# A norm moved ahead of a product, and a feed-forward piece moved to the end of a slot, in a two-layer Perceiver kernel

## The chip, the cores and the metric

The kernel runs on one core of a Trainium2 chip. The metric is the device time of one execution in microseconds (us). The core has a matrix engine (TensorE, PE in the profile, with its weight loads as PEld), VectorE (DVE), ScalarE (ACT), GpSimd (POOL) and SyncE (SP), which issues most DMA transfers. Each engine has its own queue of instructions; semaphores order them between engines.

## The reference

Sixteen sequences of 64 tokens of width 256 (1024 tokens) go through two layers, all in float32. Each layer has a cross-attention over a context of 1601 rows of width 192, a self-attention or a stand-in for it, and a feed-forward part. Each step adds to the residual stream, and each takes a layer norm of it:

```
x = x + L0_xattn(layernorm(x), ctx)     # 16 heads of 16
x = x + L0_attn(layernorm(x))           # causal self-attention, see below
x = x + L0_ffn(layernorm(x))            # gelu, 256 -> 1024 -> 256
x = x + L1_xattn(layernorm(x), ctx)     # 8 heads of 64
x = x + L1_attn(layernorm(x))           # a scan of gradient steps over sequences
x = x + L1_ffn(layernorm(x))            # mixture of experts, top 2 of 8, and a shared one
```

The self-attention is the one of the first edit:

```
q, k, v from rmsnorm(x); 16 query heads, 8 key/value heads of 64
q, k = each head's row divided by its norm, times a scale     # "heads' norms"
sim = tanh(q k / 50) * 50 / 8, causal; attn = softmax(sim)
out = sum of the two query heads of a group (attn v), then @ Wout
```

## The kernel before

The 1024 tokens lie as eight tiles `x[t]` of 128 tokens (two sequences each) by 256. The program is written as one order of pieces; each piece emits instructions on several engines, and each engine runs its own in the order in which they were written. Blocks under `manual_schedule` are not reordered. Four stages follow each other: `cross0` (0 to about 820 us), `middle` (self-attention and the first feed-forward, 820 to 1019 us), `cross1` (the second cross-attention with the scan, the router and the last feed-forward tile between its matmuls), and `experts`.

**`middle`** loops over the eight tiles. One turn of the loop is a list of pieces that belong to three tiles at once: tile t's attention, tile t-1's feed-forward (`before`), and tile t+1's projections (`after`). What matters here:

- `project(after, n)`: the products for queries (n = 0, 1), keys (n = 2) and values (n = 3), line L137 (the helper that accumulates). For n < 3 ScalarE squares the result (L1820) and VectorE sums it (L1829).
- `inverse_norms(after)`: a root on ScalarE (L1833) and a reciprocal on VectorE, 24 heads at once.
- `over_norm(after, n)`: one product on VectorE (L1838, 128 x 512), in the order n = 2, 0, 1. The three results are read by `turn_keys` (L697), `turn_queries(t, 0)` and `turn_queries(t, 1)` (L711) at the start of the next turn of the loop.
- `attention_out(t)`: a product on TensorE and the addition to `x[t]` on VectorE (L795).
- `feed.norm2(t)`: the layer norm ahead of the feed-forward: statistics on VectorE (L1435, L1437, L627), a root on ScalarE (L109), a reciprocal (L110), the scaled tile `xs` (L1444), then a bias row that GpSimd adds to `x[t]` (L132). `feed.norm3` and `make.norm1` are the same for the next layer's norm and the next tile's first norm.
- `feed.turn2(before)` transposes norm2's `xs` on TensorE (L634) and copies it on ScalarE (L637, `xt`). It stands between the two `turn_queries`. `feed.hidden` reads `xt` (L137, 32 matmul records `h`) and ends in GELUs on ScalarE (L1875); `feed.out` is L1886 and its addition L1894; `turn1(after)` transposes the next tile's first norm (L634 again).

Tile 7's `norm2` and tile 6's `norm3` are not made in `middle`; they come at the start of `cross1`.

**`cross1`** goes through 64 units v (a sequence and a pair of heads each), one slot per unit. A slot holds, in this order on TensorE: two groups of transposes of the weights of unit v-1 (L991), the main part of the scores of v (L947), the other transposes, the rest of the scores (L959), whose maxima (L971, L972, L974) and exponentials (L977 to L979) `weights` emits on VectorE and ScalarE, and the weighted sum of v-1 (L1007). Three times in a slot other work is let in:

```
place_in(v, 3.9)                 # behind the main scores
place_in(v, 1.6, long=True)      # behind weights
place_in(v, 1.6)                 # behind the weighted sum
```

Outside the last nine slots `place_in` calls `place`, which takes the next piece of `feed` (a generator) as long as it has one, and after that a piece of the scan or the router. `feed` is `FeedForward.rest()`: norm2 of tile 7 and norm3 of tile 6 (emitted ahead of the first slot), then `turn3` + `turn2`, `hidden(0)`, `hidden(1)`, `out` with norm3 of tile 7, and `turn3`. So the first slot's three places hold `turn3` + `turn2`, `hidden(0)` and `hidden(1)`; there is no v-1 in this slot, so nothing else of it lies behind `weights`.

Of the kernel before, what the change touches and what calls it, by code (L numbers as in the profile page):

```python
# [76 lines left out]
class Perceiver:  # L77
# [561 lines left out]
    def middle(self, make):  # L639
# [6 lines left out]
        with ExitStack() as ctx:  # L646
# [35 lines left out]
            def projected(name):  # L682
                return ps_q.tile([P, 512], F32, tag="q", name=name)

            feed = FeedForward(
                self, sb, psum, lambda: ps_y.tile([P, D], F32, tag="y", name="y")
            )
# [127 lines left out]
            def each(*pieces):  # L815

                for f, t, *more in pieces:
                    if 0 <= t < NT and (f, t) not in ((feed.norm2, last), (feed.norm3, last - 1)):
                        f(t, *more)

            with tc.manual_schedule():
                for t in range(NT):
                    before, after = t - 1, t + 1
                    first = last if t == 0 else NT

                    end, soon, later = (t, before, NT) if t == last else (NT, NT, before)
                    each(
                        (turn_keys, t),
                        (turn_queries, t, 0),
                        (last_of_cross0, first, 0),  # L830
                        (feed.turn2, before),
                        (turn_queries, t, 1),
                        (last_of_cross0, first, 1),
                        (feed.norm3, before - 1),
                        (make.norm1, after if t else NT),
                        (feed.hidden, before, 0),
                        (feed.hidden, before, 1),
                        (turn1, after),
                        (scores, t),
                        (feed.turn3, before - 1),  # L840
                        (feed.out, before, 0),
                        (project, after, 2),
                        (next_queries, end, -1, 0),
                        (attend, t),
                        (project, after, 0),
                        (feed.out, soon, 1),
                        (join, t),
                        (project, after, 1),
                        (next_queries, end, 0, 3),
                        (make.inverse_norms, after),  # L850
                        (make.over_norm, after, 2),
                        (make.over_norm, after, 0),
                        (attention_out, t),
                        (next_queries, end, 3, 6),
                        (make.over_norm, after, 1),
                        (feed.norm2, t),
                        (project, after, 3),
                        (feed.out, later, 1),
                        (next_queries, end, 6, 8),
                    )  # L860
                    if t == 2:
                        self.load_context(0)
# [48 lines left out]
    def cross1(self, ps_m, scan, shared, one, early):  # L911
# [7 lines left out]
        with ExitStack() as ctx:  # L919
# [7 lines left out]
            def turned(name):  # L927
# [3 lines left out]
            feed = FeedForward(  # L931
                self,
                sb,
                turned,
                lambda: ps_m.tile([P, D], F32, tag="tr", name="y"),
                ("at", "at", "pt", "p"),
            ).rest()
# [45 lines left out]
            def transposed(v, n):  # L983

                if n == 0:
                    pts[v] = sb.tile([P, NCH, P], F32, tag="pt", name="pt")
                ks = range(4 * n, min(4 * n + 4, NCH))
                w = chunk_rows(ks[0])
                t = ps_w.tile([P, 4, P], F32, tag="w", name="w")
                for k in ks:  # L990
                    nc.tensor.transpose(  # L991
                        t[:w, k - ks[0], :], ps[v][:, k * P : k * P + w], self.ident
                    )
                copy = nc.scalar.copy if n % 2 else nc.vector.tensor_copy
                copy(pts[v][:w, ks[0] : ks[-1] + 1, :], t[:w, : len(ks), :])  # L995
# [18 lines left out]
            def over_weights(v):  # L1014
                den = self.small.tile([P, 1], F32, tag="den1", name="den1")
                nc.vector.reciprocal(den, us[v][:, DC:])
                nc.vector.tensor_scalar(us[v][:, :DC], us[v][:, :DC], den, None, ALU.mult)

            def sums_by_width(v):
                b, j = divmod(v, 4)  # L1020
                if v % 8 == 0:
                    uts[b // 2] = self.early.tile([DH, 2, 8, 2, N], F32, tag="ut", name="ut")
                m = ps_m.tile([DH, 2, P], F32, tag="tr", name="m")
                for i in range(2):
                    nc.tensor.transpose(m[:, i, :], us[v][:, i * DH : (i + 1) * DH], self.ident)
                for i in range(2):
                    self.evacuate(
                        uts[b // 2][:, i, 2 * j : 2 * j + 2, b % 2, :],
                        m[:, i, :].rearrange("p (e q) -> p e q", e=2),
                    )  # L1030
# [23 lines left out]
            def place(long=False):  # L1054

                if next(feed, False) is False:
                    scan.go_on(long=long)

            def last_slots(v):
                return v >= units - 9  # L1060

            def place_in(v, us, long=False):

                if last_slots(v):
                    scan.timed(us)
                else:
                    place(long)
# [11 lines left out]
            def first_half():  # L1079
                next(first, None)  # L1080

            def table():
                nonlocal made
                if made is None:
                    made = self.table(one, *TABLES[0], self.counts[NT - 2], True)
                self.first_table = next(made)
# [5 lines left out]
            for v in range(units + 2):  # L1092
                if 0 <= v - 1 < units:
                    transposed(v - 1, 0)
                if 0 <= v - 2 < units:
                    over_weights(v - 2)
                if 0 <= v - 1 < units:
                    transposed(v - 1, 1)
                if v >= units:
                    first_half()  # L1100
                    sums_by_width(v - 2)
                if v > units:

                    table()
                    first_half()
                    values(NT - 1)
                    table()
                    first_half()
                    first_half()
                    output(NT - 1)  # L1110
                    scan.timed(3.0)
                    table()
                    for _ in range(3):
                        first_half()
                        scan.timed(0.9)
                    break
                if v < units:
                    scores_main(v)
                    if 0 <= v - 2:
                        sums_by_width(v - 2)  # L1120
                place_in(v, 3.9)
                if 0 <= v - 1 < units:
                    transposed(v - 1, 2)
                    transposed(v - 1, 3)
                if last_slots(v):
                    scan.timed(0.7)
                if v >= units:
                    first_half()
                t, m = divmod(v + 6, 8)
                if t < NT and m == 0:  # L1130
                    self.queries(t, turned)
                if t < NT and 1 <= m < 5:
                    self.queries_by_width(t, 2 * (m - 1), turned)
                if v < units:
                    scores_rest(v)
                    weights(v)
                if t < NT and 1 <= m < 5:
                    self.queries_by_width(t, 2 * (m - 1) + 1, turned)
                t, m = divmod(v - 9, 8)
                if 0 <= t < NT - 1 and m == 0:  # L1140
                    values(t)
                if 0 <= t < NT - 1 and m == 1:
                    output(t)
                place_in(v, 1.6, long=True)
                if 0 <= v - 1 < units:
                    weigh(v - 1)
                place_in(v, 1.6)
                if v == units:
                    table()
                if v % 4 == 1 and 0 < v < units - 4:  # L1150
                    self.load_context((v + 3) // 4)
                if v == 1:
                    early()

# [979 lines left out]
```

## Time and profile before

| what | value |
|---|---|
| median of three runs | 2147.42 us (2143.57, 2147.42, 2154.95) |
| profiled execution | 2142.42 us |
| its span, first to last instruction | 2140.8 us |
| mean granted TensorE clock | 0.992 |
| PE busy | 2074.3 us, 97% of the span |
| DVE busy | 1114.3 us, 52% |
| ACT busy | 682.4 us, 32% |
| POOL busy | 152.4 us, 7% |
| one tile of `middle` (from one turn_keys to the next) | 25.98 us |

The profile's line numbers are those of the kernel. `L634 MATMUL t<-ident,xs` is an instruction of line 634 that writes the tile t and reads ident and xs. In rows in order of time the first number is the start in us from the span's start, the second the length, and a bracket at the end gives the idle time of the engine just before and what ended it. A helper's line (L137, L634, L637, L1444) stands for all its callers, so position and tile names tell which one it is. A clock of 1.00 is full speed.

### The profile page before, as it was taken

The numbers are of one execution on the slowest core, as the hardware profiler recorded it, in microseconds if no ns is written. First come the engines' busy times: TensorE is split into PE (matmuls) and PEld (weight loads), VectorE is DVE, ScalarE is ACT, GpSimd is POOL, SyncE is SP. The second block draws the span as 40 slices with busy tenths as digits, with TensorE's granted clock in tenths as the row PEclk, the third lists the DMA queues.
The fourth block names the chain that finished last, engine by engine and source line by source line (L and its number), as shares of the span: only waits on it lengthen the run. The fifth ranks groups of instructions, "written<-read, shape, count | busy, mean of one in ns | idle before, by whom it ended". The sixth has DMA issues, their size and how long they took to land.

```text
span 2140.8 us, 49996 instructions
## 1 busy us (share of the span) xinstructions
PE 2074.3 (97%) x21950; PEld 1597.3 (75%) x21950; DVE 1114.3 (52%) x3088; ACT 682.4 (32%) x1258; POOL 152.4 (7%) x400
## 2 busy tenths in 40 slices
PE   8999999999999998999999999999999998989998
PEld 5777776777777776767778777778777776768897
DVE  5445454544444444555444555555555555566443
ACT  1333334333333334444322222323232222211111
POOL 3000000000000000000000000000000000011212
PEclk9999999999999999999999999999999999999999
DMA  4010000000001004000631111111111110047895
GB/s 146 27 49 29 27 27 27 27 27 27 27 27 36 27 19 143 1 1 1 172 93 47 47 49 49 47 52 47 52 47 52 47 52 29 1 167 237 263 327 168
DMA packets 86376, 146.60 MB, mean 68 GB/s; under 512 B 4397, under 2 KB 49150, under 8 KB 86158
## 3 DMA queue, kind: packets, MB, share of 16 engines
q1 hardware_dynamic: 81390, 136.27, 19.4%
q0 software_dynamic: 4768, 7.13, 1.5%
q8 instruction: 172, 2.82, 0.6%
q14 instruction: 46, 0.38, 0.1%
HBM read 128.63 MB, written 14.76 MB: 67 GB/s over the span
## 4 chain that ended last, share of the span: by engine, by line
PE 85%; DVE 9%; ACT 4%; DMA 2%; issue 1%; SPq 0%; POOLq 0%; DVEq 0%; ACTq 0%
PE u L1007 13%; PE s L947 8%; PE s L340 6%; PE w L378 6%; PE g L137 6%; PE kv L304 5%; PE w L991 5%; PE kv L274 4%; PE s L959 4%; PE o L416 3%; PE kv L316 3%; PE kv L280 3%; DVE mx L350 3%; PE y L137 2%; PE m L137 2%; PE w L388 2%
## 5 line engine op out<-in xcount | busy, mean ns | idle before, releaser
L350 DVE TENSOR_REDUCE mx<-s 128x2 f32<-128x896 f32 (+2 forms) x256 | 254.3, 993 | 209.0 <-PE s L340 204.0
L402 ACT ACTIVATE pt<-w 128x768 f32<-128x768 f32 (+1 forms) x256 | 221.2, 864 | 363.5 <-PE w L388 362.2
L1007 PE MATMUL u<-cn,pt 128*128 128x193 f32 (+1 forms) x1664 | 297.2, 332 | 1.0 <-ACT pt L995 1.0
L1007 PEld LDWEIGHTS u<-cn,pt 128*128 128x128 f32 (+1 forms) x1664 | 273.1, 190 | 21.4 <-issue 14.6
L378 PE MATMUL w<-q,kt 32*128 32x128 f32 x3328 | 254.1, 286 | 3.0 <-ACT pt L402 2.9
L340 PE MATMUL s<-kt,q 32*128 32x448 f32 (+2 forms) x1024 | 241.6, 548 | 14.2 <-DVE mx L350 9.2
L378 PEld LDWEIGHTS w<-q,kt 32*128 32x128 f32 x3328 | 205.3, 186 | 9.6 <-ACT pt L402 5.1
L947 PE MATMUL s<-ctm,qw 128*128 128x401 f32 (+1 forms) x512 | 183.2, 500 | 0.0
L325 DVE COPY vt<-kv 128x384 f32<-128x384 f32 (+1 forms) x128 | 75.0, 586 | 138.3 <-PE kv L316 138.3
L340 PEld LDWEIGHTS s<-kt,q 32*128 32x128 f32 x1024 | 76.8, 183 | 81.8 <-issue 24.1
L137 PE MATMUL g<-xst,w 128*128 128x128 f32 x1104 | 135.3, 280 | 1.1 <-DVE xst L1458 1.1
L947 PEld LDWEIGHTS s<-ctm,qw 128*128 128x128 f32 x512 | 92.2, 190 | 56.8
L137 PEld LDWEIGHTS g<-xst,w 128*128 128x128 f32 x1104 | 131.0, 195 | 4.7 <-issue 1.9
L995 DVE COPY pt<-w 128x512 f32<-128x512 f32 x128 | 88.0, 688 | 76.5 <-PE w L991 74.5
L416 PEld LDWEIGHTS o<-pt,vt 128*32 128x32 f32 x6656 | 99.8, 110 | 35.4 <-issue 35.4
L991 PE MATMUL w<-ident,p 128*128 128x128 f32 (+1 forms) x832 | 123.2, 278 | 2.4 <-ACT us L1012 1.0
L416 PE MATMUL o<-pt,vt 128*32 128x64 f32 x6656 | 120.4, 222 | 0.0
L304 PEld LDWEIGHTS kv<-wc,ctm 128*128 128x128 f32 x832 | 100.3, 196 | 19.7 <-issue 19.7
L304 PE MATMUL kv<-wc,ctm 128*128 128x128 f32 x832 | 112.7, 288 | 0.0
L288 ACT ACTIVATE kt<-kv,cols 128x448 f32<-128x448 f32 (+2 forms) x128 | 69.1, 591 | 132.8 <-PE kv L280 132.8
L991 PEld LDWEIGHTS w<-ident,p 128*128 128x128 f32 (+1 forms) x832 | 93.4, 141 | 21.6 <-ACT us L1012 10.7
L959 PE MATMUL s<-ctr,qw 64*128 64x401 f32 (+1 forms) x512 | 107.5, 520 | 0.0
(372 smaller groups left out, 2916.3 us busy)
## 6 DMA issues: line engine op xcount, KB each, us to landing
w<-in_m_w SPq DMA_DIRECT2D x23, 2304.0 KB, 11.6
cn<-in_ctx SPq DMA_DIRECT2D x16, 1152.0 KB, 12.2
ctm<-in_ctx_m SPq DMA_DIRECT2D x16, 832.0 KB, 4.5
ctm<-in_ctx_m SPq DMA_DIRECT2D x16, 800.5 KB, 4.3
rows<-none SPq DMA_DIRECT2D x1, 8385.0 KB
ctr<-in_ctx_h SPq DMA_DIRECT2D x16, 448.0 KB, 5.0
ctr<-in_ctx_r SPq DMA_DIRECT2D x16, 400.5 KB, 3.2
xs<-rows SPq DMA_DIRECT2D x19, 129.0 KB, 10.2
```

The source lines that it names most:

```text
L137: self.nc.tensor.matmul(ps, lhsT, rhs, start=i == 0, stop=i == n - 1)
L304: nc.tensor.matmul(ps[:, k - lo, :], main[:, k * P : (k + 1) * P], self.wv[:, 0, c], start=k == lo, stop=False, skip_group_check=True,)
L340: nc.tensor.matmul(s[:, i, : hi - lo], q[u % 2][r, u // 2, :], kts[u % 3][r, lo:hi], start=True, stop=True,)
L350: nc.vector.tensor_reduce(mxs[u, pp][:, :, n : n + 1], s[:, :, : hi - lo], AX.X, ALU.max)
L378: nc.tensor.matmul(w[:, i, k - lo, :], kts[u % 3][r, k * P : (k + 1) * P], q[u % 2][r, u // 2, :], start=k == lo, stop=False, skip_group_c ...
L402: nc.scalar.activation(pts[u, n][:, 2 * pp : 2 * pp + 2, : hi - lo, :], w[:, :, : hi - lo, :], AF.Exp)
L416: nc.tensor.matmul(os[u][32 * j : 32 * j + 32, e * N : (e + 1) * N], vt[:w, k, 2 * j + e, :], pt[:w, j, k - lo, e * N : (e + 1) * N], star ...
L947: nc.tensor.matmul(ss[v][n // 2][:, n % 2, : hi - lo], queries_of(v, 0), cts[v // 4][0][:, lo:hi], start=True, stop=False,)
L959: nc.tensor.matmul(ss[v][n // 2][:, n % 2, : hi - lo], queries_of(v, 1)[r, :], cts[v // 4][1][r, at : at + hi - lo], start=False, stop=True,)
L991: nc.tensor.transpose(t[:w, k - ks[0], :], ps[v][:, k * P : k * P + w], self.ident)
L995: copy(pts[v][:w, ks[0] : ks[-1] + 1, :], t[:w, : len(ks), :])
L1007: nc.tensor.matmul(u, pt[r, k, :], cn[r, k, :], start=k == 0, stop=k == NCH - 1)
```

## The change

Two pieces are moved in the written order. In `middle`, `norm2` of tile t stands ahead of the third `over_norm` of tile t+1 (n = 1) instead of behind it. In `cross1`, the first slot (v = 0) has no place behind its main scores; it gets one at its end instead. The pieces of `feed` keep their own order, so each of the slot's three places now gives the piece that the list holds next.

```diff
                         (attention_out, t),
                         (next_queries, end, 3, 6),
+                        (feed.norm2, t),
                         (make.over_norm, after, 1),
-                        (feed.norm2, t),
                         (project, after, 3),
...
                     if 0 <= v - 2:
                         sums_by_width(v - 2)
-                place_in(v, 3.9)
+
+                if v:
+                    place_in(v, 3.9)
                 if 0 <= v - 1 < units:
                     transposed(v - 1, 2)
                     transposed(v - 1, 3)
...
                 if v % 4 == 1 and 0 < v < units - 4:
                     self.load_context((v + 3) // 4)
+                if v == 0:
+                    place()
                 if v == 1:
                     early()
```

The changed lines lie at 852 to 856, 1121 and 1151 of the kernel before.

## The prediction

> **What bounds the kernel now.** I read the page's busy table first, then its chain that ended last, then the self-attention stage (820 to 1019 us) and the first slot of the second attention (1019 to 1033 us) in order of time, with the granted clock beside them.
>
> ```profile
> PE 2074.3 (97%) x21950; PEld 1597.3 (75%) x21950; DVE 1114.3 (52%) x3088; ACT 682.4 (32%) x1258; POOL 152.4 (7%) x400
> PE 85%; DVE 9%; ACT 4%; DMA 2%; issue 1%; SPq 0%; POOLq 0%; DVEq 0%; ACTq 0%
> ```
>
> TensorE is the bound over the span: only 66.5 us of 2140.8 are without a matmul. A change can win what TensorE waits in its stage, and no more than the next late thing allows. So the question is, for each moved piece, which wait of TensorE ends last there.
>
> The first edit lies at the border of two self-attention tiles. This is the border 3 to 4 in the order of time (start, length, what, and idle time before it with its releaser); the borders 1 to 2 through 5 to 6 look alike.
>
> ```profile
> 889.50 0.41 DVE L795 TENSOR_TENSOR x<-y,x 128x256 f32<-128x256 f32 x1
> 889.83 0.68 DVE L1838 TENSOR_TENSOR qk<-a,ssq 128x512 f32<-128x512 f32 x1
> 890.43 0.42 DVE L1435 BATCH_NORM_STATS2 st<-x 128x6 f32<-128x256 f32 x1
> ...
> 891.72 0.41 DVE L1444 TENSOR_SCALAR xs<-x,mv,rs 128x256 f32<-128x256 f32 x1
> ...
> 892.19 0.44 PE L634 MATMUL t<-ident,xs 128*128 128x128 f32 x2 [0.60 <-DVE xs L1444]
> ...
> 892.46 0.60 PE L711 MATMUL t<-ident,qk 128*128 128x128 f32 x4
> ...
> 893.09 3.84 PE L137 MATMUL h<-xt,ut 128*128 128x128 f32 x32
> ...
> 897.09 0.44 PE L634 MATMUL t<-ident,xs 128*128 128x128 f32 x2 [0.16 <-DVE xs L1444]
> ```
>
> TensorE stands 0.60 us until the second norm's tile xs is there (turn2), and again 0.16 us for another xs, the next tile's first norm (turn1). From the product over heads' norms at 888.29 to the xs of 895.00 and then 896.62, VectorE has no idle time but three waits of 0.27 us for ScalarE's roots. The chain of waits in this stage runs through it: L1838, L1435, L1444, then the third norm, the first norm, ScalarE's root, its table load and eight GELUs, and only then TensorE.
>
> The second edit lies in slot v = 0 of the second attention:
>
> ```profile
> 1019.27 2.96 PE L947 MATMUL s<-ctm,qw 128*128 128x401 f32 x8
> 1024.59 0.41 DVE L1444 TENSOR_SCALAR xs<-x,mv,rs 128x256 f32<-128x256 f32 x1
> 1025.05 0.66 PE L634 MATMUL t<-ident,xs 128*128 128x128 f32 x4 [2.82 <-DVE xs L1444]
> 1025.64 2.53 PE L959 MATMUL s<-ctr,qw 64*128 64x401 f32 x8
> 1025.75 0.37 ACT L637 COPY xt<-t 128x256 f32<-128x256 f32 x1 [1.39 <-PE t L634]
> 1028.10 4.55 PE L137 MATMUL h<-xt,ut 128*128 128x128 f32 x32
> 1029.24 0.15 DVE L974 TENSOR_REDUCE nm<-mx 128x1 f32<-128x2 f32 x1
> 1029.47 1.28 ACT L977 ACT_TABLE_LOAD   x1 [3.35 <-DVE nm L974]
> 1031.73 0.93 ACT L979 ACTIVATE p<-s,nm 128x800 f32<-128x800 f32 x1
> ```
>
> TensorE waits 2.82 us for two norms before it can turn their tiles; the rest of the scores (L959), which needs neither, stands behind them. The exponentials' weights come after the table load. The clock in steps of 3.4 us (busy time and count of PE, granted clock, DMA share, GB/s):
>
> ```profile
> 1022.60:1026.00 3.40, 0.95 (x6) 1.00 0.69 228
> 1026.00:1029.40 3.40, 3.40 (x14) 0.53 0.02 5
> 1029.40:1032.80 3.40, 3.40 (x31) 0.97 0.00 0
> ```
>
> The gap is followed by 3.4 us at about half clock: (0.47 + 0.03) x 3.4 = 1.7 us lost.
>
> **Edit 1: norm2 ahead of the third over_norm.** No instruction is added or removed. On VectorE the five instructions of norm2 pass one product, seven times (tiles 0 to 6; tile 7's norm2 is left to the next stage), and on ScalarE the same root keeps its place in the queue. TensorE's, POOL's and SP's orders are as before. POOL's row addition (0.74 us) starts earlier with xs and lies under VectorE work as now; L1894 and L716 take 0.42 and 0.69 us with and without it beside them, so I cost it at nothing.
>
> Worked for the border above. The addition starts at 889.50 as before. norm2 then starts 0.60 earlier (what the product of 0.68 occupies of the chain), xs is done at 891.53 instead of 892.13, and turn2 can start at 891.59 just as turn_queries(t, 0) ends: the 0.60 wait is gone. ScalarE's root, v copy and kt copy also move up by 0.6, so the xt copy follows at about 892.1. But the passed product now ends at 892.13, and turn_queries(t, 1) reads it: it waits from 892.03 to 892.19. The hidden layer starts 0.27 us earlier (892.19 instead of 892.46 ahead of it). Then the next wait takes it back: turn1 needs the first norm's xs, which stands on VectorE behind L1894, two qt products, and the third norm. Those do the same work in the same time, since VectorE was never idle. The one gain there is the second qt product: it started at 893.10, right as TensorE's turn of 893.06 ended, and alone it would start 0.60 after its forerunner's 892.38, at 892.98. So of 0.60 us, about 0.1 remains for the ScalarE chain and everything behind it; turn1's wait grows from 0.16 to about 0.35.
>
> At the border 0 to 1 there is no feed-forward output and no third norm: TensorE waits 1.83 us at turn2, the second qt product waits 0.37 us for TensorE, and turn1 waits for nothing. There 0.28 us of the move should stay. At 6 to 7 there is no turn1, but the attention of tile 7 waits for ScalarE's chain (0.50 us, for xt), which gains only the 0.1. Sum: 0.28 + 6 x 0.1 = 0.9 us gained. Bounds: nothing, if the qt products keep their starts, and 7 x 0.6 = 4.2 us, if nothing behind were late.
>
> **Edit 2: slot 0's first place moves to the slot's end.** Pieces come from a list in order, so the three calls of the slot still give turn3 + turn2, hidden(0), hidden(1); the calls are now the second, the third and a new last one. The order of instructions on TensorE shows a single move: the four transposes of turn3 and turn2 go behind the rest of the scores. But their copies move too. VectorE's xt copy (0.42) goes behind the three maxima; ScalarE's xt copy (0.37), which the hidden layer reads, goes behind the exponentials' table load and the three exponentials. No DMA moves, and no POOL instruction.
>
> Step by step. The main scores end at 1022.23. The rest follows at once at full clock: 1.62 us (what L959 x8 takes in slot 1), until 1023.85. The transposes still need xs: 1025.05 to 1025.7. VectorE, free at 1025.0, takes the maxima 0.91 + 0.98 + 0.15 and has nm at about 1027.0. ScalarE waits for nm, loads its table (1.28), and exponentiates in 0.47 + 0.47 + 0.93: from 1027.1 to 1030.2. Only then comes the xt copy, until 1030.55. The hidden layer, 1028.10 before, starts at about 1030.6. TensorE has nothing else in its queue: behind the hidden layer stand slot 1's transposes. So a gap of 2.82 us turns into one of 1.2 us for xs and one of 4.9 us for the copy.
>
> The hidden layer takes 3.84 us at full clock (all seven times in the stage before) and took 4.55 behind the old half-clock spell. **A rule and the row:** a spell after a gap is what the rows above show, and also the 2.55 us gap before 816.7, after which the clock was 0.65 and 0.85 in two steps of 3.4 us: again 1.7 us lost. The Trainium skill (TensorE: Matmul & The Clock Gate, "Why this matters for your kernels") advises against idle gaps over about 3 us. Read strictly, the old gap of 2.82 was free and only the new one costs; the trace says the old one cost 1.7 too. By the rule the edit loses 1.7 more than by the rows. I take the rows: both versions pay about one spell, 1.7 us here, with bounds 0 (the spell falls into the gap) and 3.4 (a second such step). The new hidden layer then ends at 1030.6 + 3.84 + 1.7 = 1036.1 instead of 1032.65: **3.5 us lost**, bounds 1.8 and 5.2.
>
> **A second rule:** the Trainium skill (ScalarE: Activation LUTs, "What ACT_TABLE_LOAD costs") puts a switch of tables at 1283 ns for the load and about 1380 ns for a drain. The row has the load at 1029.47 with 1.28, and the first exponential at 1030.77: no such drain behind it. With the rule's 2.66 the copy would come 1.4 us later and the loss be 4.9; I keep the row.
>
> Is the loss taken back later? Slot 1's first transposes had their p before they were reached; the GELUs follow the hidden layer through their own table load, and the output of the feed-forward followed without a wait. All of that hangs on the hidden layer and shifts with it. From there to the end TensorE is nearly gapless, so I keep the whole 3.5.
>
> **Sum.** 3.5 - 0.9 = +2.6 us. On the profiled execution (2142.42 us, of which 2140.8 the span and 1.6 around it) that makes 2145.0. The three runs shown have a median of 2147.42, 5.0 us above the profiled one, and spread over 11 us; on that median the forecast is **2150.0 us**, +0.12%. About 0.5%, 10.7 us, is what a measurement of this kernel can tell from no change, so "no change" is the call, leaning slower.
>
> **Rivals.**
> - *The self-attention wait is really won.* If turn1's wait does not grow, 7 x 0.6 = 4.2 us are gained, the net is 3.5 - 4.2 = -0.7 us: 2146.7. For it: turn2's wait is the longest on TensorE there at each border. Against: VectorE's queue is full until turn1's xs. Chance 0.12.
> - *The gap in slot 0 simply closes.* If the copy did not hold the hidden layer, it would start at 1026.1 and end warm at 1029.95, 2.7 us early; with edit 1, -3.6 us: 2143.8. For it: the 2.82 us gap. Against: ScalarE ran in written order everywhere in the trace, and the copy is written behind the exponentials. Chance 0.08.
> - *Slower: the clock gives way in the self-attention tiles.* One tile (956.8 to 963.6) had 0.67 and 0.83 of the clock with no gap above 1 us, after a step of 3.4 us with 2.67 us busy. If the lengthened wait at turn1 puts a step of each of the six later tiles under that mark, 6 x 1.7 = 10 us are lost: +12.8 us, 2160.2. It decides from about 0.7 us idle in a step. Against: idle time per tile is not increased, only moved, and five tiles with the same 0.60 + 0.16 waits stayed at 1.00. Chance 0.09.
>
> **How the numbers follow.** The forecast has 0.71. Its own range: the loss from 1.8 to 5.2 and the gain from 0 to 1.9 (7 x 0.27, if each earlier start of the hidden layer stays) give 2147.3 to 2152.6, and a median of three such runs moves by several us, so 2143 to 2157. Taking in the first rivals and part of the last: 2142 to 2158. Faster by over 0.5% would need more than all gains together, 0.03; slower by over 0.5% is the last rival or the runs' spread, 0.10; the rest 0.87.
>
> **What would show it.** In the changed profile: turn2's 0.60 us wait gone at six borders, a short wait at turn_queries(t, 1), turn1's wait grown to 0.3 to 0.45, and the period of a tile (25.98 us between turn_keys) less by about 0.1. In slot 0: L959 right behind L947 with about 1.6 us, the transposes still at xs, the hidden layer waiting some 5 us for ScalarE's xt, a half-clock spell in it. Wrong if the hidden layer starts within 1 us of the transposes, if the period falls by 0.3 or more, or if a second spell appears in the tiles.

## The result and the profile after

The changed kernel took 2153.81 us (median of 12 runs, 2146.06 to 2157.65) against 2147.65 us for the kernel before (12 runs, 2143.57 to 2154.95). The ratio is 1.0028, with a 95% interval of 1.0017 to 1.0040: some 6 us slower, between 3.6 and 8.6. Measured once more beside before, it was 1.0021 (1.0007 to 1.0036), 4.5 us. Both lie within the 0.5% that the prediction called no change, on its slower side, and above its +2.6.

The profiled execution took 2149.87 us, with a span of 2148.3 us. The span is 7.5 us longer than that of the profiled execution of before, but not all of it belongs to the change. The first turn_keys of self-attention stands at 825.28 us instead of 820.98, and nothing ahead of it was changed: 4.3 us of the 7.5 are a difference between two executions of the same instructions, with the clock lower in the first slice of the page's PEclk row (8 instead of 9). From there to slot 0's main scores it took 200.40 us instead of 198.29, but a second profile of the same kernel took 198.90, so these 2.1 us come and go as well. What the change did has to be read as distances inside its own stages.

The same border of self-attention in order of time (the prediction called it 3 to 4; in the kernel's own numbers, from 0, it lies between tiles 2 and 3):

```profile
894.18 0.41 DVE L795 TENSOR_TENSOR x<-y,x 128x256 f32<-128x256 f32 x1
894.63 0.43 DVE L1439 BATCH_NORM_STATS2 st<-x 128x6 f32<-128x256 f32 x1
...
895.93 0.41 DVE L1448 TENSOR_SCALAR xs<-x,mv,rs 128x256 f32<-128x256 f32 x1
...
896.26 0.68 DVE L1842 TENSOR_TENSOR qk<-a,ssq 128x512 f32<-128x512 f32 x1
...
896.40 0.44 PE L634 MATMUL t<-ident,xs 128*128 128x128 f32 x2
...
897.09 0.63 PE L711 MATMUL t<-ident,qk 128*128 128x128 f32 x4 [0.25 <-DVE qk L1842]
...
897.56 3.74 PE L137 MATMUL h<-xt,ut 128*128 128x128 f32 x32
...
901.77 0.44 PE L634 MATMUL t<-ident,xs 128*128 128x128 f32 x2 [0.47 <-DVE xs L1448]
```

The 0.60 us wait at turn2 is gone. In its place stand 0.25 us at turn_queries(t, 1), which now waits for the passed product, and turn1's wait has grown from 0.16 to 0.47. The turn_keys that follow come 25.98 or 25.99 us apart, as before, but for one distance in each of the two profiles (27.69 here, 27.64 before) in which TensorE ran a stretch at half clock.

Slot 0 of the second attention, in order of time:

```profile
1025.68 2.96 PE L947 MATMUL s<-ctm,qw 128*128 128x401 f32 x8
...
1028.57 1.62 PE L959 MATMUL s<-ctr,qw 64*128 64x401 f32 x8
...
1031.53 0.66 PE L634 MATMUL t<-ident,xs 128*128 128x128 f32 x4 [1.34 <-DVE xs L1448]
...
1033.54 1.28 ACT L977 ACT_TABLE_LOAD   x1 [2.71 <-DVE nm L974]
...
1035.80 0.93 ACT L979 ACTIVATE p<-s,nm 128x800 f32<-128x800 f32 x1
1036.61 0.38 ACT L637 COPY xt<-t 128x256 f32<-128x256 f32 x1
...
1037.05 5.23 PE L137 MATMUL h<-xt,ut 128*128 128x128 f32 x32 [4.86 <-ACT xt L637]
...
1042.12 1.04 PE L991 MATMUL w<-ident,p 128*128 128x128 f32 x8
```

The rest of the scores fills 1.62 us of the old gap at full clock. Then TensorE waits 1.34 us for xs and 4.86 us for ScalarE's copy, which ScalarE reaches only behind its table load and three exponentials. From the main scores to slot 1's first transposes it takes 1042.12 - 1025.68 = 16.44 us. Before, slot 1's first transposes were

```profile
1032.49 1.04 PE L991 MATMUL w<-ident,p 128*128 128x128 f32 x8
```

and the distance 1032.49 - 1019.27 = 13.22. That is 3.2 us more. Behind slot 0 nothing comes back: from slot 1's first transposes to slot 2's it takes 14.09 us here and 14.10 before, and from the main scores of slot 1 to those of slot 58 it takes 756.65 to 756.68 us in all ten profiles of this document. Only behind that do the two profiles part, mostly by half-clock stretches, three single ones before and one of double length here: from slot 1's transposes to the end it takes 1106.2 us here and 1108.3 before.

The clock in steps of 3.4 us (busy time and count of PE, granted clock, DMA share, GB/s):

```profile
1028.80:1032.20 3.40, 2.05 (x12) 1.00 0.67 231
1032.20:1035.60 3.40, 0.00 (x0) 0.64 0.02 9
1035.60:1039.00 3.40, 1.95 (x9) 0.50 0.00 0
1039.00:1042.40 3.40, 3.40 (x28) 0.85 0.00 0
```

The half clock begins inside the gap and lasts into the hidden layer, which takes 5.23 us instead of 3.84, 1.4 us more than at full clock. With the stretches laid on its edges, it is half (0.50) from 1033.17 to 1040.00 us and full on both sides. Before, half clock had its price in slot 0 too: the rest of the scores took 2.53 us instead of 1.62, and the hidden layer 4.55 instead of 3.84, 1.6 us together.

### The profile page after: what moved, and what is told of

Same layout as the page of the kernel before. It is cut to its first block, busy times and chain, and to the rows that moved or that the text cites. A ratio compares the mean times of both kernels' runs of the same rounds, so it can differ in the third digit from the quotient of the medians.

```text
span 2148.3 us, 50002 instructions
## 1 busy us (share of the span) xinstructions
PE 2079.3 (97%) x21950; PEld 1601.1 (75%) x21950; DVE 1114.4 (52%) x3088; ACT 683.3 (32%) x1258; POOL 153.0 (7%) x400
## 3 DMA queue, kind: packets, MB, share of 16 engines
q8 instruction: 172, 2.82, 0.5%
## 4 chain that ended last, share of the span: by engine, by line
PE 85%; DVE 9%; ACT 4%; DMA 2%; issue 1%; SPq 0%; POOLq 0%; DVEq 0%; ACTq 0%
PE u L1007 13%; PE s L947 8%; PE s L340 6%; PE w L378 6%; PE g L137 5%; PE kv L304 5%; PE w L991 5%; PE kv L274 4%; PE s L959 4%; PE o L416 3%; PE kv L316 3%; PE kv L280 3%; DVE mx L350 3%; PE y L137 3%; PE m L137 2%; PE a L137 2%
## 6 DMA issues: line engine op xcount, KB each, us to landing
w<-in_m_w SPq DMA_DIRECT2D x23, 2304.0 KB, 10.9
```

## The experiments

Each was timed against before on the same chip; a kernel had 12 runs beside 28 to 35 of before (11 and 6 runs for the last two). The theory: edit 1 moves a wait, because VectorE's queue, ScalarE's root, table load and GELUs set the period of a tile; edit 2 loses because it puts ScalarE's xt copy behind the exponentials, and the gap then takes TensorE's clock. The rival was that the extra loss beyond slot 0 comes from edit 1, by half-clock spells in self-attention.

**The first edit alone.**

```diff
+                        (feed.norm2, t),
                         (make.over_norm, after, 1),
-                        (feed.norm2, t),
```

> The first edit alone: norm2 ahead of the third over_norm, slot 0 as before. Theory (the tile's period is set by VectorE's queue, ScalarE's root, the table load and the GELUs, and VectorE only swaps two pieces): period 25.98 us unchanged, time within 1 us of before. Rival (the longer wait at turn1 puts more stretches of self-attention under the half clock): +2.5 to +3 us, which is what the two edits cost together beyond slot 0, with more half-clock spells between 845 and 1020 us than before has.

Ratio 0.9997 (0.9985 to 1.0009): nothing, at most 1.9 us slower or 3.2 faster. The rival's +2.5 to +3 is outside. The period, in TensorE's part of the order of time:

```profile
891.50 0.60 PE L697 MATMUL t<-ident,qk 128*128 128x128 f32 x4
...
917.49 0.60 PE L697 MATMUL t<-ident,qk 128*128 128x128 f32 x4
...
943.48 0.60 PE L697 MATMUL t<-ident,qk 128*128 128x128 f32 x4
...
971.16 0.60 PE L697 MATMUL t<-ident,qk 128*128 128x128 f32 x4
```

25.99 us at full clock, as predicted by the theory and 0.1 off the prediction's own figure. The fourth row stands 27.68 us behind the third: TensorE ran 3.4 us of it at half clock. In this profile there are three such stretches between 845 and 1020 us, where that of before has one. So the rival's sign came, though its loss did not. It is no sign of edit 1: a profile further down that leaves self-attention as it was (the rest of the scores first) has four, and the granted clock averages 0.9895 over these 12 runs and 0.9892 over the 35 of before.

**The second edit alone.**

```diff
+                if v:
                     place_in(v, 3.9)
...
+                if v == 0:
+                    place()
```

> The second edit alone: slot 0's first place moved to its end. Theory (the loss is the hidden layer held by its xt copy behind the exponentials): from the main scores of slot 0 to slot 1's first transposes 16.4 us instead of 13.2, time +3 us. Rival (the whole measured difference of +6 us comes from this edit, by later effects): +6 us.

Ratio 1.0017 (1.0005 to 1.0030): 3.7 us slower, between 1.1 and 6.4, which rules out neither +3 nor +6. Slot 0 in order of time:

```profile
1019.80 2.96 PE L947 MATMUL s<-ctm,qw 128*128 128x401 f32 x8
...
1031.13 6.08 PE L137 MATMUL h<-xt,ut 128*128 128x128 f32 x32 [4.86 <-ACT xt L637]
...
1037.05 1.04 PE L991 MATMUL w<-ident,p 128*128 128x128 f32 x8
```

17.25 us, 4.0 more than before. The same 4.86 us wait as with both edits, but this execution paid more for the clock: the hidden layer took 6.08 us, 2.2 more than at full speed. In both the half clock lasts 6.83 us. Here it begins at 1029.03, 2.1 us ahead of the hidden layer, and with both edits at 1033.17, 3.9 us ahead of it; what falls into the gap costs nothing. The place of the half-clock spell differs from execution to execution, so this edit's price does too.

**The two edits again.** The kernel is the changed one, unedited.

> Both edits together, measured again beside before. Theory (slot 0's loss of 3 to 4 us, nothing from the first edit, the rest of the first measured +6 is how many half-clock spells happened to fall into the runs): +3 to +4.5 us. Rival (the two edits cost more together than one by one, by spells in self-attention): +6 us again.

Ratio 1.0021 (1.0007 to 1.0036), 4.5 us; in slot 0 it took 1038.59 - 1021.39 = 17.20 us, 4.0 more than before, with a hidden layer of 6.11. So the theory's +3 to +4.5 and the first +6 are both in reach of this interval, the rival's extra cost is not needed, and it is not ruled out to the last microsecond.

**The rest of the scores first, without moving the copies.** This keeps what edit 2 wins and leaves out what it costs.

```diff
+                if v == 0:
+                    scores_rest(v)
                 place_in(v, 3.9)
...
                 if v < units:
-                    scores_rest(v)
+                    if v:
+                        scores_rest(v)
                     weights(v)
```

> In slot 0 the rest of the scores goes ahead of the first place, but the place stays ahead of the maxima and exponentials, so that both xt copies keep their place in VectorE's and ScalarE's queues. First edit left out. Theory: TensorE fills 1.6 us of the 2.82 us gap, waits about 1.2 us for xs, the hidden layer starts near 1026.1 on the scale of before (1028.1) and mostly at full clock; 2 to 3.5 us are won against before, and 5 to 7 against the second edit alone. Rival (the wait for xs alone is what costs, whatever stands behind it): within 1 us of before.

Slot 0 in order of time:

```profile
1026.04 2.96 PE L947 MATMUL s<-ctm,qw 128*128 128x401 f32 x8
...
1031.70 0.66 PE L634 MATMUL t<-ident,xs 128*128 128x128 f32 x4 [1.16 <-DVE xs L1447]
...
1032.40 0.37 ACT L637 COPY xt<-t 128x256 f32<-128x256 f32 x1 [1.40 <-PE t L634]
...
1032.83 3.84 PE L137 MATMUL h<-xt,ut 128*128 128x128 f32 x32 [0.46 <-ACT xt L637]
...
1036.50 1.04 PE L991 MATMUL w<-ident,p 128*128 128x128 f32 x8
```

10.46 us instead of 13.22: 2.8 us won in the slot, of which 2.0 are the hidden layer's earlier start and 0.7 its full clock. Against edit 2 alone it is 6.8 us. The only difference between the two in the queues is where the copies stand to the maxima and the exponentials. The ratio, 0.9991 (0.9977 to 1.0006), agrees with that gain but does not tell it from none: the runs spread over 13 us. The slot's own time settles it: in the four profiles whose slot 0 is as before it takes 13.08 to 13.22 us.

One more thing helped, and the theory did not have it:

```profile
1032.79 1.28 ACT L977 ACT_TABLE_LOAD   x1
...
1034.63 0.60 ACT L977 ACTIVATE p<-s,nm 128x401 f32<-128x401 f32 x1 [0.56 <-DVE nm L974]
```

Before, this table load waited for the maxima's nm like the exponentials behind it; here it runs ahead of nm, right behind the copy. So the exponentials end at 1036.53, just as slot 1's transposes start; with the load behind nm they would end about 1.3 us later (an estimate from the load's 1.28 us). A copy stands ahead of the load before as well (1025.75), so why it waits there and not here stays open.

**Filling edit 2's gap.** The lines shown are added to those of the second edit.

```diff
                 place_in(v, 1.6, long=True)
+                if v == 0:
+                    spare = ps_w.tile([P, 4, P], F32, tag="w", name="warm")
+                    for _ in range(20):
+                        nc.tensor.matmul(
+                            spare[:, 0, :], self.ident, self.ident, start=True, stop=True
+                        )
```

> The second edit alone, with 20 products of the identity with itself put on TensorE in slot 0 between the transposes and the hidden layer, into a PSUM tile that nothing reads, so that TensorE is busy in the gap. Theory (the hidden layer starts when ScalarE's xt copy is done, and 1.4 to 2.2 us of the loss is the half clock that the gap brings): the hidden layer starts as late as before the fill, takes 3.84 us instead of 5.2 to 6.1, and from slot 0's main scores to slot 1's transposes it takes about 15 us: +1.8 us against before. Rival (the half clock does not hang on this gap): 16.4 us or more, +3 us.

First the slot in TensorE's order of time, then the clock:

```profile
1018.94 2.96 PE L947 MATMUL s<-ctm,qw 128*128 128x401 f32 x8
...
1025.14 4.63 PE L1149 MATMUL warm<-ident 128*128 128x128 f32 x40
1030.16 3.84 PE L137 MATMUL h<-xt,ut 128*128 128x128 f32 x32 [0.40 <-ACT xt L637]
1033.84 1.04 PE L991 MATMUL w<-ident,p 128*128 128x128 f32 x8
```

```profile
1025.70:1029.10 3.40, 3.40 (x33) 1.00 0.01 5
1029.10:1032.50 3.40, 3.00 (x27) 1.00 0.00 0
```

The hidden layer still starts 11.2 us behind the main scores (11.3 without the fill), held by the copy, but takes 3.84 us at full clock. Slot 0 takes 14.90 us: 1.7 more than before, and 1.5 to 2.4 less than with the gap open. Since before lost 1.6 us of its 13.22 to its own half clock, the copy's delay alone costs about 14.90 - (13.22 - 1.6) = 3.3 us (an estimate, with full clock on both sides). The half clock behind the new gap takes the place of that behind the old one and adds little to the difference. The ratio, 1.0012 (0.9999 to 1.0026), does not separate the two expectations (+1.8 and +3); the slot does.

**The norms ahead of the second query product.** The experiment on edit 1's mechanism: take work out of VectorE's queue ahead of norm1.

```diff
-                        (turn_queries, t, 1),
-                        (last_of_cross0, first, 1),
                         (feed.norm3, before - 1),
                         (make.norm1, after if t else NT),
+                        (turn_queries, t, 1),
+                        (last_of_cross0, first, 1),
```

> Self-attention: norm3 and norm1 go ahead of turn_queries(t, 1), so that on VectorE they stand ahead of the second qt product; norm2 and slot 0 as before. Theory (root, table load and GELUs behind VectorE's queue set the period): the root of norm1 comes 0.6 to 0.7 us earlier, the period falls from 25.98 to about 25.3 us, and six tiles win about 4 us in all. Rival (VectorE's sum of work is the bound, whatever the order): period 25.98, no gain.

Ratio 0.9974 (0.9959 to 0.9989): 5.6 us won (2.4 to 8.8), so the rival, no gain, is out. In order of time, the same border, with the GELUs' table load, which stands behind norm1's root:

```profile
893.31 0.60 PE L697 MATMUL t<-ident,qk 128*128 128x128 f32 x4
...
894.95 0.44 PE L634 MATMUL t<-ident,xs 128*128 128x128 f32 x2 [0.60 <-DVE xs L1444]
...
898.43 1.28 ACT L1875 ACT_TABLE_LOAD   x1
...
918.56 0.60 PE L697 MATMUL t<-ident,qk 128*128 128x128 f32 x4
```

Before, the turn_keys and the table load of that border were

```profile
890.55 0.60 PE L697 MATMUL t<-ident,qk 128*128 128x128 f32 x4
...
896.40 1.28 ACT L1875 ACT_TABLE_LOAD   x1
```

The table load stands 5.12 us behind turn_keys instead of 5.85 (896.40 - 890.55), and the period is 25.25 us: 0.73 less for a product of 0.68 taken out ahead. The 0.60 us wait at turn2, which edit 1 removes, is still there, and did not matter.

**The third product behind the norms too.**

```diff
-                        (turn_queries, t, 1),
                         (last_of_cross0, first, 1),
                         (feed.norm3, before - 1),
                         (make.norm1, after if t else NT),
                         (feed.hidden, before, 0),
                         (feed.hidden, before, 1),
+                        (make.over_norm, t if t else NT, 1),
+                        (turn_queries, t, 1),
...
-                        (make.over_norm, after, 1),
...
-                m = psum("t")
+                m = projected("t") if n else psum("t")
```

> Self-attention: the third product over heads' norms, turn_queries(t, 1) and its product go behind norm2, norm3 and norm1 (turn_queries(t, 1) takes a PSUM tile of the projections' pool for it); slot 0 as before. Theory (the period is set by root, table load and GELUs behind VectorE's queue, so that what is taken out of the queue ahead of norm1 counts in full): 0.7 us for the query product and 0.6 us for the third product, period about 24.7 us, some 8 us won. Rival (after 0.7 us another wait ends last, the transposes behind the hidden layer or the scores' PSUM tile): period near 25.3, 4 to 5 us won, no more than with the norms moved alone.

Ratio 0.9958 (0.9945 to 0.9972): 9 us won (6.0 to 11.8). In order of time:

```profile
893.07 0.60 PE L697 MATMUL t<-ident,qk 128*128 128x128 f32 x4
...
897.73 1.28 ACT L1875 ACT_TABLE_LOAD   x1
...
898.27 0.68 DVE L1838 TENSOR_TENSOR qk<-a,ssq 128x512 f32<-128x512 f32 x1
...
899.01 0.66 PE L711 MATMUL t<-ident,qk 128*128 128x128 f32 x4
...
917.94 0.60 PE L697 MATMUL t<-ident,qk 128*128 128x128 f32 x4
```

The table load comes 4.66 us behind turn_keys, and the period is 24.88 us on the mean (24.87 in these rows), 1.10 below before; the rival's 25.3 is out. Of the 0.6 us for the product, 0.4 arrived. The statistics now start 0.45 us behind the addition; with the product between them it was 0.93 before (889.50 to 890.43). So only 0.48 was there to win, and the last 0.1 is not explained. From the first turn_keys to slot 0 the profile is 6.3 us shorter; between 845 us and slot 0 it has no stretch at half clock, while each of the eight profiles above has one to four. Edit 1's idea, to let norm2 pass this product, pays once norm1 passes it as well.

**All that won, together.** The order of the last kernel, the rest of the scores first in slot 0, and the subtraction of the scan's weights (L1166, behind a transfer) moved behind slot 0's two norms on VectorE.

```diff
             next(feed)
+            self.subtract_steps()
             for v in range(units + 2):
...
         self.nc.gpsimd.dma_start(self.b1, a["t_b1"].partition_broadcast(P))
+
+    def subtract_steps(self):
         self.nc.vector.tensor_tensor(
```

> The self-attention order with the product behind, the rest of slot 0's scores ahead of its first place, and the subtraction of the scan's weights, which waits for a transfer, behind the two norms of that slot on VectorE. Theory: xs comes 1 to 1.6 us earlier, slot 0 loses its gap and its half-clock spell; from main scores to slot 1's transposes about 9.3 us instead of 13.2; with the self-attention's 8 us, 11 to 12 us won. Rival (slot 0's norms wait for something else, so the subtraction hides nothing): 10.5 us in slot 0, 9 to 11 us won in all.

Slot 0 in order of time:

```profile
1012.40 2.96 PE L947 MATMUL s<-ctm,qw 128*128 128x401 f32 x8
...
1015.29 1.62 PE L959 MATMUL s<-ctr,qw 64*128 64x401 f32 x8
...
1016.95 0.66 PE L634 MATMUL t<-ident,xs 128*128 128x128 f32 x4
...
1018.07 3.84 PE L137 MATMUL h<-xt,ut 128*128 128x128 f32 x32 [0.46 <-ACT xt L637]
...
1021.75 1.04 PE L991 MATMUL w<-ident,p 128*128 128x128 f32 x8
```

9.35 us instead of 13.22, with no wait for xs left, as the theory had it and not the rival. Ratio 0.9944 (0.9927 to 0.9962): 12 us won (8.2 to 15.7), 2134.12 us; by itself that would fit both. This version beats both kernels.

## Why the prediction was right or wrong

- *No change within 0.5%, leaning slower:* right. The size was off: +2.6 forecast, +6.0 and +4.5 measured.
- *Edit 2's step, 3.5 us with bounds of 1.8 and 5.2:* right in mechanism and, with some luck, in size. The order of waits, 1.2 us for xs and 4.9 for the copy, was 1.34 and 4.86. Three executions lost 3.2, 4.0 and 4.0 us. The term for the half clock, 1.7 us, measured 1.4, 2.2 and 2.3 on the hidden layer; the fill showed that it belongs to the gap. The luck is in this term: it stood for one step of 3.4 us that lies wholly on the hidden layer, while all three executions had two such steps and lost the first for the most part in the gap. The row was also the right side of the first rule: each of the four profiles that have the old gap (2.70 to 2.82 us) has a half-clock step of 3.41 us within 1.6 us behind it, and with the gap cut to 1.16 us, in one profile, the hidden layer ran at full clock. Behind the table load, the first exponential of the changed kernel started at 1034.83, 0.01 us after its end; no drain, as the row had it. Nor is there one ahead of a load: before, a norm's root on ScalarE ends at 896.38 us and the GELUs' load starts at 896.40.
- *Edit 1's step, "So of 0.60 us, about 0.1 remains":* this is the term that was mis-sized. It measured 0.0. Its main claim held: turn2's wait went and came back at turn1, where it grew to 0.47 and not 0.35. Its expected 0.1 was lost in a place it had not looked at. Before, the addition (L795) and the statistics that read its result (L1435) stood with the product between them, and the product's row followed the addition after 0.33 us. Now they are neighbours, and the statistics follow after 0.45 us. That the distance hangs on the reading, and not on the statistics, is seen before, where they follow a tile that they do not read after 0.33 us:

```profile
895.00 0.41 DVE L1444 TENSOR_SCALAR xs<-x,mv,rs 128x256 f32<-128x256 f32 x1
895.33 0.42 DVE L1435 BATCH_NORM_STATS2 st<-x 128x6 f32<-128x256 f32 x1
```

  These 0.12 us take the 0.12 that the second query product gained. At the border 0 to 1, where 0.28 were expected, turn_keys to turn_keys measured 25.21 us against 25.22: the passed product ended later by the same 0.13, TensorE waited 0.25 us for it, and norm1's root came 0.02 us earlier only. Behind the last turn_keys, where 0.1 were expected, the second profile of the changed kernel took 23.14 us to slot 0, before 23.12.
- *The sum:* with 0 in place of -0.9 it is 3.2 to 4.0 us. The measured 4.5 (1.5 to 7.7) holds that, and so, barely, does the interval of the 6.0 (3.6 to 8.6). What is left of the 6.0 is open. It is not edit 1, unless the two work together in a way that neither shows alone; the spread of half-clock spells over a run is large enough (the 12 runs of the changed kernel go from 2146.06 us at a mean clock of 0.991 to 2157.65 at 0.986).
- *The rivals:* the wait that is really won fell with the unchanged period; the closing gap fell with the 4.86 us wait. The spells in the tiles come with and without edit 1, none to four in a profile, and edit 1's runs are no slower for them. That rival's mark, about 0.7 us idle in a step, does not decide: before, TensorE is busy for 2.68 us in each of the steps of 3.41 us from 875.99, 927.21 and 954.52 us, and only the third is followed by half clock.

## What to carry to other kernels

A wait that is removed pays only if the chain that ends last runs through it: here TensorE's 0.60 us wait was fed by VectorE's queue, and swapping two pieces of that queue moved it, while taking a piece out ahead of the root on which ScalarE's table load waits paid 0.7 us a tile. When a piece is moved, follow its copies as well as its matmuls: the transposes lost nothing by standing later, the copy behind them came 4.5 us later (10.9 us behind the main scores instead of 6.5) because on its engine it fell behind a table load and three exponentials. Price a new TensorE gap by its own length and by the clock behind it, and take off what the old gap cost.

## What the runs showed of the hardware that was not expected

On VectorE, a 128 x 256 instruction of 0.41 us is followed by one that does not read its result after 0.33 us (889.50 to 889.83, 895.00 to 895.33) and by one that reads it after 0.45 us (894.18 to 894.63 in the changed kernel). A TensorE gap of 1.16 us ahead of the transposes left the clock at full speed in its one profile, one of 2.70 to 2.82 us did not in any of four, and identity products that nothing reads kept it at 1.00 through a stretch of 4.9 us. In self-attention and slot 0 the granted clock was full or half, and a half-clock stretch lasted 3.41 us or two or three times that; before, two of them start at 957.93 and 1026.20 us, 20 times 3.41 us apart.
